# Packing every sign convolution two output channels to a weight, with the precision check moved out of the main path

## The chip, the core and the metric

The program runs on one core of a Trainium2 chip. The metric is the device time of the whole launch in microseconds; the kernel before takes 1131.07 us (median of three runs, 1129.95 to 1135.38). The engines that matter are TensorE (matmuls, and the weight loads that go with them), ScalarE (activations; ACT in the profile), VectorE (DVE), GpSimd (POOL) and the DMA queues. They run side by side and wait for one another through semaphores.

## What is computed

Four layers are applied to x of shape (16, 256, 28, 28): 16 images, 256 channels, 784 pixels. Cut to what matters here:

```python
# layer 0: 3x3 convolution of signs by signs, batch norm, residual
y = conv3x3(sign(x), sign(w0)) * mean(|w0|)
x = batchnorm(y) + x
# layer 1: 3x3 and 1x1 convolutions with real weights, gates, PReLU (not touched by the change)
# layer 2: two more sign-by-sign convolutions
o = sign(batchnorm(x));  o = prelu(conv3x3(o, sf1 * sign(w1)), a1)
o = sign(batchnorm(o));  o = prelu(conv3x3(o, sf2 * sign(w2)), a2)
x = prelu(batchnorm(o) + x, a3)              # prelu(v, a) = v if v >= 0 else a * v
# layer 3: single-head attention over the 784 pixels, softmax, projection, residual
x = x + Wp @ softmax(q^T k / 8) v
```

Batch norm takes mean and variance over all images, so a layer must be finished for every image before the next can start. In a sign-by-sign convolution each output is a whole number of magnitude at most 2304 (256 channels by 9 taps).

## The kernel before

The 256 input channels are two blocks of 128 (k), the 256 outputs two blocks of 128 (mo), and a 3x3 convolution is nine shifted matmuls per block. An image is worked in two halves of 392 pixels; `j` counts the 32 half images. The nine taps by two blocks make six chunks `n` of three taps.

Five of the six chunks are *packed*: the weight `4095 * sign(w of channel o+128) + sign(w of channel o)` gives two output channels in one matmul, `4095 b + a`. To take it apart, ScalarE computes `r = ps/4095` plus a large constant, so that the addition rounds to the whole number b; VectorE subtracts the constant; and two more matmuls, by matrices -4095 I and I, add `-4095 b` to the packed sum (which leaves a) and put b in the second bank. The sixth chunk is *plain*, so that the packed sum cannot grow beyond what fp32 holds exactly: three matmuls for each of the two output blocks.

```python
    def sign_layer(pads, w, temp, sign, post, steps, moments, first=None, together=1):
        def packed(*js):
            for j in js:
                pss[j] = conv_ps()                        # two PSUM banks, three such pairs in all
            for n in range(5):
                for j in js:
                    for t in range(3):
                        product(j, 0, w[0][:, n, t, :], n, t, n + t == 0, n + t == 6)
            for j in js:
                r, bs[j] = temp("t1"), temp("uv", FR)
                A.activation(r, pss[j][:, 0, :HN], AF.Identity, bias=rounding, scale=1.0 / PACK)
                V.tensor_scalar(bs[j], r, -ROUND, None, ALU.add)
        def plain(j):
            for mo in range(2):
                for t in range(3):
                    product(j, mo, w[1][:, t, mo * P:(mo + 1) * P], 5, t, ...)
            for mo in range(2):
                T.matmul(pss[j][:, mo, :HN], lhsT=unpack[mo], rhs=bs[j], ...)
        ...
            for j in range(2 * B + 1):                    # cut: the order of the engines' work
                packed(j)
                if j > 0:
                    plain(j - 1); post(j - 1, pss[j - 1])
                sign_image(j // 2 + 1)                    # every second j: signs of the next image
                if j == 2 * B - 2: moments.gather()
                if late: late()
                late = steps.pop(0)() if j >= 2 and steps else None   # weights of the next layers
```

After that `post` takes what it needs from PSUM. In layer 0 it is two `bn_stats` and an int16 copy; in layer 2 the PReLU as `y + (1 - a) * relu(-y)` and the statistics:

```python
            def post0(j, ps):                             # layer 0
                for mo in range(2):
                    V.bn_stats(mom.part(j, mo), ps[:, mo, :HN])
                A.copy(ns[b][:, :, h * HN:(h + 1) * HN], ps[:, :, :HN])
                def post(j, ps):                          # layer 2, both convolutions
                    A.activation(r[:, mo], ps[:, mo, :HN], AF.Relu, scale=-1.0)
                    for mo in range(2):
                        V.scalar_tensor_tensor(p, r[:, mo], beta[:, mo:mo + 1], ps[:, mo, :HN], ALU.mult, ALU.add)
                        V.bn_stats(mom.part(j, mo), p)
```

Beside layer 0 run the `steps`: six that prepare layer 1's weights (`w1_step`: ten VectorE and four ScalarE operations), six sums of |w0|, one for the 1x1 weights, one for constants, and five of the six chunks of the next sign layer's weights. Matmuls on zeros (`keep_busy`) fill the gaps between layers.

The attention begins with layer 2's last norm, residual and PReLU for each image (`finish_a`, `_b`, `_c`). From image 2 on the residual is added by a DMA that accumulates into SBUF. The finished image is also stored to DRAM (`xd`), for a second version of the attention that runs in a branch if the exponentials overflowed:

```python
    def finish_a(b, ...):   # ACT: norm; b < 2: DVE adds x2; b >= 2: DMA with accum adds x2d
    def finish_b(b, ...):   # ACT: rl = relu(-x)
    def finish_c(b, ...):   # DVE: x = rl * (1 - a3) + x;  SP: dma xd[b] <- x
        for b in range(B - 1):                            # cut
            scores(b, 1)
            if b == 0: finish_b(1); finish_c(1)
            sum_up(b, 1); scores(b, 2); scores(b, 3); sum_up(b, 2, 3)
            queries_keys(b + 1, ...); keys_to(...); queries(...)
            if b == 0: finish_a(2)
            project_v(b + 1); turn_v(b + 1)
            scores(b, 4); scores(b, 5); sum_up(b, 5)
            finish_b(b + 2); finish_c(b + 2); finish_a(b + 3)
            for c in range(4): values(b, c)
            ...
```

Of the kernel before, what the change touches and what calls it, by code (L numbers as in the profile page):

```python
# [35 lines left out]
P = 128  # L37
# [12 lines left out]

ROUND = 1.5 * 2**23
# [12 lines left out]

@with_exitstack
def conv_seq_kernel(ctx: ExitStack, tc: tile.TileContext, d: dict, out: bass.AP):
# [28 lines left out]
    CHUNKS = [(k, g) for g in range(3) for k in range(2)]  # L95

    unpack = [wpool.tile([P, P], FR, name=f"unpack{i}") for i in range(2)]
    rounding = const.tile([P, 1], F32, name="rounding")
# [22 lines left out]
    class Moments:  # L121


        def __init__(self, name, early, late, early_count):
            self.parts = const.tile([P, 2, early, 6], F32, tag="parts", name=name + "_parts")
            self.fin = const.tile([P, 2, 3 + 6 * late], F32, name=name + "_fin")
            self.mv = const.tile([P, 2, 2], F32, name=name + "_mv")
            self.early, self.count = early, float(early_count)
# [4 lines left out]
        def gather(self):  # L133

            nc.gpsimd.memset(self.fin[:, :, 0:1], self.count)
            for k in range(2):
                V.bn_aggr(self.fin[:, k, 1:3], self.parts[:, k].rearrange("p c s -> p (c s)"))
            V.tensor_scalar(self.fin[:, :, 2:3], self.fin[:, :, 2:3], self.count, None, ALU.mult)

# [32 lines left out]
    def packed_weights(pool, **kw):  # L172
        return pool.tile([P, 5, 3, P], FR, name="wpk", **kw)

    def plain_weights(pool, **kw):
        return pool.tile([P, 3, 256], FR, name="wpl", **kw)
# [14 lines left out]
    def sign_weights(pool, dst, src, total, acc, stage=("st", 2), tmp=None, ab_tag="rn", sg=("sg", 1)):  # L191
# [9 lines left out]
        def sign(k, g):  # L201
            st = sts[k, g]
            n = CHUNKS.index((k, g))
            if n == 5:
                A.activation(dst[1], st, AF.Sign, saturate=False)
                return lambda: None
# [3 lines left out]
                dst[0][:, n], t[:, :, P:], PACK, t[:, :, 0:P], ALU.mult, ALU.add  # L210
# [33 lines left out]
    def sign_layer(pads, w, temp, sign, post, steps, moments, first=None, together=1):  # L244
# [4 lines left out]
        bs = [None] * 2 * B  # L249

        def product(j, mo, lhsT, n, t, start, stop, again=False):
            k, g = CHUNKS[n]
            r, c = divmod(3 * g + t, 3)
            r += HR * (j % 2)
            T.matmul(  # L255
                pss[j][:, mo, :HN].rearrange("p (a b) -> p a b", b=S), lhsT=lhsT,
                rhs=pads[:, j // 2 % 2, k, r:r + HR, c:c + S], start=start, stop=stop, skip_group_check=again,
            )

        def packed(*js):  # L260
            for j in js:
                pss[j] = conv_ps()
            for n in range(5):
                for j in js:
                    for t in range(3):
                        product(j, 0, w[0][:, n, t, :], n, t, n + t == 0, n + t == 6)
            for j in js:
                r, bs[j] = temp("t1"), temp("uv", FR)
                A.activation(r, pss[j][:, 0, :HN], AF.Identity, bias=rounding, scale=1.0 / PACK)  # L269
                V.tensor_scalar(bs[j], r, -ROUND, None, ALU.add)  # L270

        def plain(j):
            for mo in range(2):
                for t in range(3):
                    product(j, mo, w[1][:, t, mo * P:(mo + 1) * P], 5, t, mo == 1 and t == 0, False, mo == 0)
            for mo in range(2):
                T.matmul(  # L277
                    pss[j][:, mo, :HN], lhsT=unpack[mo], rhs=bs[j], start=False, stop=True, skip_group_check=(mo == 0)
                )
# [7 lines left out]
        with tc.manual_schedule(engines={ET.PE, ET.Activation, ET.DVE, ET.SP}):  # L287
            for j in range(2 * B + 1):
                if j == 0:
                    sign_image(0)  # L290
                    if first:
                        first()
                if j == 0:
                    packed(*range(together))
                elif together <= j < 2 * B:
                    packed(j)
                if j > 0:
                    plain(j - 1)
                    post(j - 1, pss[j - 1])
                if j == 0:  # L300
                    sign_image(1)
                elif j % 2 == 0 and j // 2 + 1 < B:
                    sign_image(j // 2 + 1)
# [4 lines left out]
                late = steps.pop(0)() if j >= 2 and steps else None  # L308
        assert not steps and not late
# [18 lines left out]
    w0 = [packed_weights(wpool, tag="wa"), None]  # L328
# [13 lines left out]
    with tc.tile_pool(name="ps_conv", bufs=3, space=PSUM) as psc, \  # L342
# [13 lines left out]
        with tc.tile_pool(name="ph1", bufs=1) as ph:  # L356

            fpads = float_pads(ph, "vs")
            w0[1] = plain_weights(ph, tag="z2", bufs=1)
# [18 lines left out]
            def temp(tag, dt=F32):  # L378
                return ph.tile([P, HN], dt, tag=tag, name=tag, bufs=2)
# [15 lines left out]
            eye = ph.tile([P, P], F32, tag="rn", name="eye", bufs=4)  # L395
            make_identity(nc, eye)
            for u, f in zip(unpack, (-PACK, 1.0)):
                V.tensor_scalar(u, eye, f, None, ALU.mult)
            nc.gpsimd.memset(rounding, ROUND)
# [58 lines left out]
            def constants():  # L458
                v = const.tile([P, 4, 2], F32, name="v_bn")
# [26 lines left out]
            w2a = [packed_weights(wpool, tag="wa2"), None]  # L486
            signs2, sums2 = sign_weights(xpool, w2a, d["w2a"], sf1, pss, ("x2", 3), tmp=ph)

            steps = load_ahead(steps + both(signs2, sums2)[:5], 2)
# [5 lines left out]
            def post0(j, ps):  # L495
# [3 lines left out]
                for mo in range(2):  # L499
                    V.bn_stats(mom.part(j, mo), ps[:, mo, :HN])  # L500
                A.copy(ns[b][:, :, h * HN:(h + 1) * HN], ps[:, :, :HN])  # L501
# [355 lines left out]
            with tc.manual_schedule(engines={ET.PE, ET.DVE, ET.Activation}):  # L857
                sc0, bi0 = norm("l0", mom, pv("g0"), pv("b0"), sf0, first)
                zb1 = tt(vtile("zb1"), bi0, pv("a_move"), ALU.add)
# [91 lines left out]
        with tc.tile_pool(name="ph2", bufs=1) as ph:  # L951
            w2b = [packed_weights(ph, tag="wb"), plain_weights(ph, tag="wbl")]
            w2a[1] = plain_weights(ph, tag="wal")
            fpads = float_pads(ph, "fpads")

            def temp(tag, dt=F32):
                return ph.tile([P, HN], dt, tag=tag, name=tag, bufs=2)

            rest = [x[5] for x in sign_weights(ph, w2a, d["w2a"], sf1, pss, ("r", 2), ab_tag="ab")]
            rest[0].load()  # L960
# [26 lines left out]
            r1, r2 = combine("r1", pv("a1"), -1.0, 1.0), combine("r2", pv("a2"), -1.0, 1.0)  # L987

            def post2(order, beta, mom):

                def post(j, ps):
                    i, h = divmod(j, 2)
                    r = ph.tile([P, 2, HN], F32, tag="r", name="r", bufs=2)
                    for mo in (slice(0, 1), slice(1, 2)) if j == 2 * B - 1 else (slice(0, 2),):
                        A.activation(r[:, mo], ps[:, mo, :HN], AF.Relu, scale=-1.0)  # L995
                    for mo in range(2):
                        p = pt[order[i]][:, mo, h * HN:(h + 1) * HN]
                        V.scalar_tensor_tensor(p, r[:, mo], beta[:, mo:mo + 1], ps[:, mo, :HN], ALU.mult, ALU.add)  # L998
                        V.bn_stats(mom.part(j, mo), p)
                return post  # L1000

            steps = both(*sign_weights(xpool, w2b, d["w2b"], sf2, pss, ("x2", 3), tmp=ph, ab_tag="ab"))
# [560 lines left out]
```

## Time and profile before

| stretch of the span, us | what runs | PE busy | DVE busy | ACT busy | granted clock |
|---|---|---|---|---|---|
| 10.70 to 153.50 | layer 0, sign convolution | 142.64 | 81.33 | 78.70 | 1.00 |
| 161.40 to 497.00 | layer 1 | 335.60 | 303.61 | 237.51 | 1.00 |
| 538.00 to 676.00 | layer 2, first sign convolution | 137.97 | 87.52 | 74.73 | 1.00 |
| 688.00 to 827.00 | layer 2, second sign convolution | 139.00 | 82.49 | 73.99 | 1.00 |
| 842.00 to 877.00 | attention, its start | 25.38 | 11.79 | 17.41 | 0.76 |
| 877.00 to 1100.00 | attention, images 2 to 14 | 223.00 | 161.59 | 168.30 | 1.00 |

The profiled execution has a span of 1132.2 us. Each row gives the length of time that each engine was executing something within that stretch; an engine whose busy time equals the stretch never paused. The granted clock is the share of full speed at which TensorE was allowed to run.

### The profile page before, as it was taken

To read this page: it belongs to the slowest core of one execution; us is meant where nothing else is said; L and a number is where in the kernel's file an instruction comes from. 1 tells how busy PE (TensorE), PEld (TensorE's weight loads), DVE (VectorE), ACT (ScalarE), POOL (GpSimd) and SP (SyncE) were. 2 spreads that over 40 slices of the span, in tenths; PEclk is the share of its full clock that TensorE was granted. 3 is DMA by queue.
4 is the path that set the end of the run, shared out by engine and by line. 5 is a ranking of instruction groups with operands and counts; after the bars stand their busy time and mean duration, and the time that the engine had idled before them with its cause. 6 is when DMAs were issued, how large, how long until landed. Compare 5 with 4: busy or idle time off the path is not lost.

```text
span 1132.2 us, 16021 instructions
## 1 busy us (share of the span) xinstructions
PE 1097.7 (97%) x6139; PEld 917.0 (81%) x6139; DVE 807.4 (71%) x1460; ACT 712.5 (63%) x1065; POOL 139.0 (12%) x140
## 2 busy tenths in 40 slices
PE   6999999999999999998999999999986999999996
PEld 6999989999999999994999998999942444444442
DVE  4766369899999999967576565565663677777865
ACT  5555445777777777766465544555554777877762
POOL 2000000000000000001000000000002444344331
PEclk9999999999999999998999999999997999999998
DMA  8554331222321222012560000000004356446522
GB/s 319 203 180 160 129 118 55 72 86 75 126 86 71 100 100 71 29 58 116 196 271 1 1 1 1 1 1 1 1 29 103 90 150 167 128 133 171 147 83 116
DMA packets 26662, 111.64 MB, mean 99 GB/s; under 512 B 3458, under 2 KB 7236, under 8 KB 26580
## 3 DMA queue, kind: packets, MB, share of 16 engines
q1 hardware_dynamic: 20948, 80.01, 19.2%
q0 software_dynamic: 5632, 30.54, 10.0%
q8 instruction: 50, 0.82, 0.3%
q14 instruction: 32, 0.26, 0.1%
HBM read 65.59 MB, written 44.96 MB: 98 GB/s over the span
## 4 chain that ended last, share of the span: by engine, by line
PE 92%; DVE 3%; ACT 2%; issue 1%; DMA 1%; POOL 0%; SPq 0%; ACTq 0%; POOLq 0%; DVEq 0%
PE cv L255 33%; PE cv L599 25%; PE sc L1180 7%; PE av L1201 7%; PE cv L705 4%; PE mi L1157 4%; PE cv L277 3%; PE unused L354 2%; PE sm L1243 2%; PE mi L1259 2%; PE sm L1201 1%; PE sumabs L222 1%; DMA p<-x2d 1%; PE hid L527 1%; PE gate L676 1%
## 5 line engine op out<-in xcount | busy, mean ns | idle before, releaser
L599 PE MATMUL cv<-vs,w 128*128 128x392 f32 x1536 | 301.3, 354 | 0.0
L255 PE MATMUL cv<-fpads,wpk 128*128 128x392 f32 x1440 | 292.0, 355 | 8.5 <-DVE wpk L209 8.3
L599 PEld LDWEIGHTS cv<-vs,w 128*128 128x128 f32 x1536 | 287.1, 190 | 1.6 <-issue 0.3
L255 PEld LDWEIGHTS cv<-fpads,wpk 128*128 128x128 f32 x1440 | 270.6, 191 | 11.0 <-POOL worst L1044 7.8
L998 DVE SCALAR_TENSOR_TENSOR p<-r,r,cv 128x392 f32<-128x392 f32 x128 | 78.5, 613 | 78.5 <-ACT r L995 78.5
L255 PE MATMUL cv<-fpads,wpl 128*128 128x392 f32 x576 | 124.9, 353 | 0.2 <-ACT t L269 0.2
L255 PEld LDWEIGHTS cv<-fpads,wpl 128*128 128x128 f32 x576 | 108.7, 190 | 1.1 <-ACT t L269 0.5
L269 ACT ACTIVATE t<-cv,rounding 128x392 f32<-128x392 f32 x96 | 56.1, 585 | 80.1 <-PE cv L255 77.9
L1184 ACT ACTIVATE es<-sc 128x784 f32<-128x784 f32 x112 | 87.3, 822 | 23.9 <-PE sc L1180 23.0
L1180 PE MATMUL sc<-q,keyswa 64*128 64x392 f32 x448 | 91.6, 521 | 3.0 <-issue 2.4
L995 ACT ACTIVATE r<-cv 128x784 f32<-128x784 f32 (+1 forms) x66 | 52.9, 805 | 56.6 <-PE cv L277 55.2
L1201 PE MATMUL av<-es,v 128*64 128x392 f32 x448 | 81.6, 503 | 5.7 <-ACT es L1184 5.7
L270 DVE TENSOR_SCALAR uv<-t 128x392 fp32r<-128x392 f32 x96 | 35.0, 365 | 71.5 <-ACT t L269 71.4
L1180 PEld LDWEIGHTS sc<-q,keyswa 64*128 64x128 f32 x448 | 39.5, 189 | 47.2 <-issue 27.8
L1201 PEld LDWEIGHTS av<-es,v 128*64 128x64 f32 x448 | 29.4, 137 | 53.4 <-issue 46.8
L1194 POOL TENSOR_TENSOR sum<-sum,es 128x784 f32<-128x784 f32 x32 | 68.0, 2126 | 3.4 <-ACT es L1184 1.0
L104 DVE TENSOR_TENSOR vs<-pad 128x840 fp32r<-128x840 bf16 (+1 forms) x66 | 64.4, 999 | 0.1
L501 ACT CAST n<-cv 128x784 int16<-128x784 f32 x32 | 26.0, 812 | 54.3 <-DVE l_parts L500 18.9
L1168 DVE COPY keyswa<-mi 64x392 f32<-64x392 f32 x31 | 16.3, 564 | 56.0 <-ACT q L1164 56.0
L745 POOL DMA_DIRECT2D x2d<-x x16 | 8.5, 532 | 356.9 <-DVE x L739 294.1
L1157 PE MATMUL mi<-p,wqk 128*128 128x392 f32 x124 | 47.4, 525 | 3.5 <-DVE p L1147 3.5
L705 PE MATMUL cv<-z,fw 128*128 128x392 f32 x256 | 49.2, 343 | 0.8 <-ACT z L697 0.7
(271 smaller groups left out, 1654.4 us busy)
## 6 DMA issues: line engine op xcount, KB each, us to landing
xs<-in_x_dram SPq DMA_DIRECT2D x30, 784.0 KB, 4.3
x2d<-x POOLq DMA_DIRECT2D x16, 784.0 KB, 3.6
xd<-p SPq DMA_DIRECT2D x16, 784.0 KB, 3.3
out_dram<-p SPq DMA_DIRECT2D x15, 784.0 KB, 6.4
p<-x2d POOLq DMA_DIRECT2D x14, 784.0 KB, 8.3
p<-x2d SPq DMA_DIRECT2D x13, 784.0 KB, 7.7
n0d<-n POOLq DMA_DIRECT2D x16, 392.0 KB, 2.7
n<-n0d SPq DMA_DIRECT2D x16, 392.0 KB, 2.9
```

Of the source, the lines that this page charges most:

```text
L104: V.tensor_tensor(o, a, b, op)
L255: T.matmul(pss[j][:, mo, :HN].rearrange("p (a b) -> p a b", b=S), lhsT=lhsT, rhs=pads[:, j // 2 % 2, k, r:r + HR, c:c + S], start=start, s ...
L269: A.activation(r, pss[j][:, 0, :HN], AF.Identity, bias=rounding, scale=1.0 / PACK)
L599: T.matmul(ps.rearrange("p (a b) -> p a b", b=S), lhsT=w[:, k, c, u, mo * P:(mo + 1) * P], rhs=vs[:, b % 2, u, k, :, c:c + S], start=(n == 0),
L705: T.matmul(ps[:, h, :HN], lhsT=w[:, k, mo * P:(mo + 1) * P], rhs=z2[b][:, k, h * HN:(h + 1) * HN], start=(k + i == 0), stop=(k + i == 2),)
L995: A.activation(r[:, mo], ps[:, mo, :HN], AF.Relu, scale=-1.0)
L998: V.scalar_tensor_tensor(p, r[:, mo], beta[:, mo:mo + 1], ps[:, mo, :HN], ALU.mult, ALU.add)
L1157: T.matmul(ps[:, h, :HN], lhsT=wqk[:, k, :], rhs=x[b][:, k, h * HN:(h + 1) * HN], start=(k == 0), stop=(k == 1))
L1180: T.matmul(ps[:, h, :HN], lhsT=chunk[rows], rhs=qs[b][rows], start=True, stop=True)
L1184: A.activation(e, ps[:, :, :HN], AF.Exp, scale=0.125)
L1194: (V if late else nc.gpsimd).tensor_tensor(sums[b, late], sums[b, late], e, ALU.add)
L1201: T.matmul(ps[64 * h:64 * h + 64, :HN], lhsT=w, rhs=e[:, h, :], start=start, stop=stop)
```

## The change

All six chunks become packed; the plain products and the two unpacking matmuls go. ScalarE now rounds and then subtracts the constant (two activations), and VectorE computes `a = ps - 4095 b` into SBUF beside b. `post` works from SBUF. The packed sum can now, for extreme data, exceed what comes apart exactly; the kernel therefore gathers sums of squares of a (layer 0: from the statistics, on GpSimd; layer 2: a ScalarE `Square` with accumulation per half image), and at the end, together with the overflow test of the attention, decides whether a whole careful version of the network (`careful=True`: two groups of three chunks, and the shifted attention) must run in a branch. With the given inputs that branch is not taken.

PReLU becomes `max(a * y, y)`, one VectorE operation, without the relu on ScalarE (it needs slopes of at most 1, which the test includes). The store of `xd` goes out of the main path. In the attention's start, the norm of image 2 and its accumulating DMA are issued earlier, the residual add and PReLU of image 1 are earlier in VectorE's order, and eight idle matmuls are put in.

```diff
+def conv_seq_kernel(tc, d, out):
+    again = forward(tc, d, out, False)
+    with tc.If(again > 0):
+        forward(tc, d, out, True)
...
-        return pool.tile([P, 5, 3, P], FR, name="wpk", **kw)
+        return pool.tile([P, 6, 3, P], FR, name="wpk", **kw)
...
+        groups = 2 if careful else 1
+        size = 6 // groups
+        def products(*js):
+            for j in js:
+                pss[j] = conv_ps()
+            for n, (k, g) in enumerate(CHUNKS):
+                for j in js:
+                    for t in range(3):
+                        T.matmul(pss[j][:, n // size, :HN]..., lhsT=w[:, n, t, :], rhs=pads[...], ...)
+        def apart(j):
+            for g in range(groups):
+                t, ab, ps = temp("t1"), temp(), pss[j][:, g, :HN]
+                A.activation(t, ps, AF.Identity, bias=rounding, scale=1.0 / PACK)
+                A.activation(ab[:, 1], t, AF.Identity, bias=unrounding)
+                V.scalar_tensor_tensor(ab[:, 0], ab[:, 1], -PACK, ps, ALU.mult, ALU.add)
...
+            sign_image(0)
+            for j in range(2 * B):
+                products(j)
+                if j % 2 == 0 and j // 2 + 1 < B:
+                    sign_image(j // 2 + 1)
+                if j > 0:
+                    post(j - 1, abs_[j - 1])
+                if j == 2 * B - 2: moments.gather()
+                if late: late()
+                late = steps.pop(0)() if j >= 2 and steps else None
+                apart(j)
+            post(2 * B - 1, abs_[2 * B - 1])
...
-                    V.bn_stats(mom.part(j, mo), ps[:, mo, :HN])
-                A.copy(ns[b][:, :, h * HN:(h + 1) * HN], ps[:, :, :HN])
+                    V.bn_stats(mom.part(j, mo), ab[:, mo])
+                A.copy(ns[b][:, :, h * HN:(h + 1) * HN], ab)
...
-                        A.activation(r[:, mo], ps[:, mo, :HN], AF.Relu, scale=-1.0)
-                        V.scalar_tensor_tensor(p, r[:, mo], beta[:, mo:mo + 1], ps[:, mo, :HN], ALU.mult, ALU.add)
+                            V.scalar_tensor_tensor(p, y, alpha[:, mo:mo + 1], y, ALU.mult, ALU.max)
                         V.bn_stats(mom.part(j, mo), p)
+                    if not careful:
+                        A.activation(temp("t2"), ab[:, 0], AF.Square, scale=SAFE**-0.5, accum_out=doubt[:, j:j + 1])
...
-    A.activation(rls[k][:, n], x[b][:, k, n], AF.Relu, scale=-1.0)
-    V.scalar_tensor_tensor(v, rls[k][:, n], na3[:, k:k + 1], v, ALU.mult, ALU.add)
-    nc.sync.dma_start(out=xd[b], in_=x[b])
+            V.scalar_tensor_tensor(v, v, alpha[:, k:k + 1], v, ALU.mult, ALU.max)
...                                                       # attention, order at its start
+        keep_busy(8)
         ...
-            if b == 0: finish_b(1); finish_c(1)
+            if b == 0: finish_a(2)                        # finish_b(1) now stands before the loop
```

All six chunks of the second sign layer's weights are now prepared beside layer 0; before, the sixth was loaded and prepared at the start of layer 2.

## The prediction

> **What bounds the kernel now.** I read the page's first part and its chain, then the busy times cut by stage, then the groups of the sign layers by shape, then the timelines of each engine inside one stage. The page says that TensorE is busy all but 3% of the span and makes up nearly all of the chain:
>
> ```profile
> PE 1097.7 (97%) x6139; PEld 917.0 (81%) x6139; DVE 807.4 (71%) x1460; ACT 712.5 (63%) x1065; POOL 139.0 (12%) x140
> PE 92%; DVE 3%; ACT 2%; issue 1%; DMA 1%; POOL 0%; SPq 0%; ACTq 0%; POOLq 0%; DVEq 0%
> ```
>
> The busy times by stage (columns: PE, weight loads, DVE, ACT, POOL, clock, DMA share, GB/s) show where there is room beside TensorE. Rows: layer 0, layer 1, the two sign convolutions of layer 2, the attention's start, the attention's steady part.
>
> ```profile
> 10.70:153.50 142.80, 142.64 (x768) 141.61 (x769) 81.33 (x207) 78.70 (x129) 8.15 (x15) 1.00 0.52 188
> 161.40:497.00 335.60, 335.60 (x1836) 334.19 (x1836) 303.61 (x569) 237.51 (x332) 7.95 (x17) 1.00 0.22 78
> 538.00:676.00 138.00, 137.97 (x738) 135.66 (x738) 87.52 (x172) 74.73 (x97) 0.00 (x0) 1.00 0.25 96
> 688.00:827.00 139.00, 139.00 (x737) 137.81 (x738) 82.49 (x157) 73.99 (x96) 0.00 (x0) 1.00 0.00 1
> 842.00:877.00 35.00, 25.38 (x142) 10.73 (x142) 11.79 (x11) 17.41 (x25) 8.31 (x6) 0.76 0.32 80
> 877.00:1100.00 223.00, 223.00 (x1474) 103.84 (x1476) 161.59 (x161) 168.30 (x281) 96.35 (x54) 1.00 0.49 136
> ```
>
> In the three sign stages DVE and ACT are busy 53 to 63% of the time, and weight loads follow each other without a gap. So time falls with the number of matmuls until another engine takes over. In layer 1 and the steady attention nothing on TensorE changes. The pitch comes from the timeline of TensorE in the last sign convolution, one half image:
>
> ```profile
> 729.90 3.00 PE L255 MATMUL cv<-fpads,wpk 128*128 128x392 f32 x15
> 732.74 1.29 PE L255 MATMUL cv<-fpads,wpl 128*128 128x392 f32 x6
> 733.87 0.52 PE L277 MATMUL cv<-uv,unpack 128*128 128x392 f32 x2
> 734.22 2.99 PE L255 MATMUL cv<-fpads,wpk 128*128 128x392 f32 x15
> ```
>
> From 729.90 to 734.22 are 4.32 us for 23 matmuls: 0.188 each (the 355 ns of the group is a modelled, pipelined end). The groups give the other engines' prices:
>
> ```profile
> L269 ACT ACTIVATE t<-cv,rounding 128x392 f32<-128x392 f32 x96 | 56.1, 585 | 80.1 <-PE cv L255 77.9
> L998 DVE SCALAR_TENSOR_TENSOR p<-r,r,cv 128x392 f32<-128x392 f32 x128 | 78.5, 613 | 78.5 <-ACT r L995 78.5
> L999 DVE BATCH_NORM_STATS2 l2c_parts<-p 128x6 f32<-128x392 f32 x58 | 33.0, 569 | 2.0
> L968 ACT ACTIVATE fpads<-p,l2b_c,l2b_r 128x784 fp32r<-128x784 f32 x30 | 29.6, 1037 | 0.0
> ```
>
> **What the Trainium skill says.** "TensorE: Matmul & The Clock Gate", section "Back-to-back issue gap", has the spacing in a real stream set by weight load and matmul together; here the loads last 190 ns and the pitch is 188, so it agrees in kind. "ScalarE: Activation LUTs", section "What ACT_TABLE_LOAD costs", gives 186 ns + 0.833 ns per element, 93 ns more for each per-partition operand, and 93 ns of overlap back to back. For 392 elements with a bias that is 606; the trace has 585 from PSUM. The new subtraction reads SBUF; a plain 392-element activation from SBUF takes 531 here, so I estimate 531 + 93 = 624, some 0.6 us after overlap. "TensorE: Matmul & The Clock Gate", section "HAM oscillation", says that TensorE's idle gaps lower its clock; the clock of 0.76 in the attention's start agrees.
>
> **The change, part by part.** *Matmuls:* 15 + 6 + 2 = 23 become 18 a half image, 18 x 0.188 = 3.39 us instead of 4.33. Over 3 x 32 half images this is 96 x 0.94 = 90 us, if TensorE remains the bound.
>
> *Load of the others in layer 2, per half image.* ACT: rounding 0.6, subtraction 0.6, half of an image's signs (1.97 for the pair back to back) 0.98, square 0.45 + 0.19 for its accumulator: 2.85. DVE: 0.6 for a, two pairs of PReLU and statistics at 1.14 a pair in the timeline: 2.9. Both stay under 3.39. There is also a chain across them. In an even half image ACT does signs 1.97, square 0.65, rounding and subtraction 1.2; in the odd one it waits for DVE's a (0.7), then 0.65 and 1.2. Together 6.5 us a pair with semaphores, against 6.8 on TensorE. So TensorE is still the bound, barely. *Second convolution:* TensorE works from 687.92 to 826.84, 138.9 us; after, 32 x 3.39 = 108.5: 30.4 gained. *First convolution:* 537.44 to 681.13, 143.7, which includes six half images that took 4.95 because DVE also prepares weights. After: 108.5 + 6 x 0.36 for the sums by TensorE + some 1 us. In those six DVE needs 2.9 + 1.6 = 4.5 against 3.75, falls behind by 4.5 us in all, and the three pairs of PSUM banks hide all but about 1. 111.7: 32.0 gained.
>
> *Tails of layer 2:* after the last matmul there are now rounding, subtraction, a, then the last PReLUs and statistics behind the aggregation. I count 5.2 us to the last statistic where the timeline has 4.0: 1.2 lost in each convolution.
>
> *Layer 0:* 10.69 to 154.72, 144.0 us. TensorE after: 108.5 + 12 x 0.36 = 112.8. But the six `w1_step`s come every second half image. DVE then has, per pair, 3.2 for the step, 1.0 for a sum, four statistics 2.0, two a 1.2: about 7.5; ACT has signs 1.5, two int16 copies 1.5, four weight copies 1.2, unpacking 2.4, waits 0.8: about 7.5. TensorE has 7.15. With their mutual waits I take 7.6: 6 x 0.45 = 3 us. The constants, some thirty small DVE operations, cost 2 more. 118: 26 gained, less 1.6 because the last statistics come 1.9 us later, partly under idle matmuls: 24.5.
>
> *Attention.* In steady state nothing: TensorE is full, and the relu that leaves ACT and the stores that leave the queue were beside it. The start is another matter:
>
> ```profile
> 853.20 4.29 PE L1157 MATMUL mi<-p,wqk 128*128 128x392 f32 x6 [1.60 <-DVE p L1147]
> 868.61 1.60 ACT L1142 ACTIVATE rl<-p 128x784 f32<-128x784 f32 x2 [5.43 <-DMA p<-x2d]
> 872.83 1.57 PE L1201 MATMUL av<-es,v 128*64 128x392 f32 x4 [5.74 <-ACT es L1184]
> ```
>
> ACT's queue stands behind image 2's accumulating DMA, issued only at 861.68, and the exponentials behind it hold up TensorE. After the change that DMA is issued about 12 us earlier and only DVE waits for it. From the value projection of image 1 (857.42) to that of image 2 (880.63) are 23.2 us, against 16.4 in steady state: 6.8 gained. Image 1's PReLU (two operations of 2.27 us on DVE while POOL adds, 1.11 alone) moves ahead of the wait: some 4.5. Together 11, the higher clock included.
>
> *Small things:* the checks' few GpSimd operations and one reduction lie beside other work; a branch not taken existed before. Zero.
>
> Sum: 24.5 + (32.0 - 1.2) + (30.4 - 1.2) + 11 = 95.5. From 1131.1 this leaves 1035.6; I add 3.5 for small waits that such counts leave out: 1039.
>
> **Rivals.** *A: ACT and DVE become the bound.* The chain of 6.5 us against 6.8 leaves 4%. If the subtraction or the square costs 0.2 more, the pair takes 7.0 to 7.2: 16 x 0.3 = 5 us in each of two or three stages, 1045 to 1055. For it: the first convolution was already DVE-bound in six half images. Against: overlap of back-to-back activations, which the timeline shows (0.47 between starts of a 0.57 activation). *B: layer 0 is held by its side work throughout*, at 4.0 per half image: about 128, 10 us more, 1049. For it: ACT's and DVE's sums are within 5% of TensorE's there. Against: only 12 of 32 half images carry the heavy steps. *C: the attention gains nothing at its start*, because image 1's PReLU still collides with POOL: 1050. *D: it also profits from a clock that stays up*, 4 us more: 1035.
>
> **Range and chances.** A, B and C each cost about 10; two of them together give 1060. All gains and D give 1030. For a time within 2% of the old one, nearly 75 of the 90 us would have to vanish, which only an engine 20% above TensorE could do. So 1024 to 1062; faster 0.97, same 0.02, slower 0.01.
>
> **What would show it.** TensorE's starts of half images 3.4 us apart in the second convolution of layer 2, weight loads still without gaps: right. A pitch of 3.6 or more, with TensorE waiting for PSUM (released by the DVE operation that makes a): A. Layer 0's pairs at 7.6 for the first twelve half images and 6.8 at the end: right; above 8 throughout: B. No wait for the DMA in the attention's start and a clock near 1: right. The prediction as a whole would be wrong if the new activations took much over 0.6 us, or if the second program's presence slowed the first.

## The result and the profile after

The changed kernel takes 1044.1 us (median of four runs, 1042.43 to 1045.54) where the kernel before takes 1130.86 (four runs, 1129.95 to 1135.38): a ratio of 0.9225, with a 95% interval of 0.9197 to 0.9253. The prediction was 1039 with a range of 1024 to 1062. The profiled executions have spans of 1132.2 and 1042.2 us, so they differ by 90.0, where the medians differ by 86.8; the stages below are read from these two. The profiled execution of the kernel before took 1134.12 us, 3.3 above its median (mean granted clock 0.986; executions of 1130.06 and 1130.53 us had 0.991), so that some 3 of the 90.0 us belong to that execution and not to the change; in which stage, the traces don't show.

The page of the changed kernel, its busy times and its chain by engine:

```profile
PE 1007.5 (97%) x5667; PEld 827.9 (79%) x5667; DVE 826.0 (79%) x1460; ACT 729.8 (70%) x1189; POOL 139.4 (13%) x147
...
PE 82%; DVE 9%; ACT 6%; issue 1%; DMA 1%; SPq 0%; POOL 0%; ACTq 0%; POOLq 0%; DVEq 0%
```

472 matmuls are gone (5667 against 6139: 480 fewer in the convolutions, eight idle ones more) and TensorE is still busy 97%. But its share of the chain fell from 92% to 82%, and VectorE and ScalarE together hold 15% instead of 5%: somewhere TensorE no longer sets the time alone. The busy times by stage say where. Columns: length, PE, weight loads, DVE, ACT, POOL, granted clock, DMA share, GB/s. Rows: layer 0, layer 1, the two sign convolutions of layer 2, the attention's start, its steady part.

```profile
10.30:131.80 121.50, 117.50 (x618) 113.06 (x619) 90.95 (x212) 99.58 (x161) 9.49 (x19) 1.00 0.66 226
139.80:476.00 336.20, 336.17 (x1840) 335.05 (x1841) 304.71 (x570) 237.89 (x334) 7.20 (x15) 1.00 0.23 78
515.00:632.80 117.80, 114.37 (x604) 112.37 (x602) 96.38 (x176) 85.80 (x160) 1.01 (x2) 0.99 0.30 116
640.80:750.00 109.20, 109.20 (x576) 108.46 (x576) 87.89 (x154) 82.80 (x155) 0.00 (x0) 1.00 0.00 1
765.00:789.00 24.00, 23.39 (x161) 10.59 (x163) 11.50 (x13) 17.52 (x25) 11.08 (x7) 1.00 0.39 68
789.00:1009.00 220.00, 220.00 (x1468) 102.54 (x1470) 162.41 (x161) 147.21 (x253) 92.60 (x53) 1.00 0.36 89
```

In the second convolution of layer 2 TensorE is busy 109.20 of 109.20. In layer 0 and in the first convolution it pauses 4.0 and 3.4 us. The attention's start now has a clock of 1.00 where it had 0.76.

The timeline of TensorE cut where one stage's first matmul starts gives the ledger (a gap is the time from one layer's last sign matmul, where the idle matmuls begin, to the next layer's first product):

| stretch | before | after | change | predicted |
|---|---|---|---|---|
| layer 0, sign convolution | 144.03 | 121.54 | -22.5 | -26.0 |
| gap to layer 1 | 6.45 | 8.03 | +1.6 | +1.6 |
| layer 1 and its end | 376.27 | 375.28 | -1.0 | 0 |
| layer 2, first sign convolution | 143.69 | 117.65 | -26.0 | -32.0 |
| gap | 6.79 | 8.00 | +1.2 | +1.2 |
| layer 2, second sign convolution | 138.92 | 109.29 | -29.6 | -30.4 |
| gap to the first query product | 9.94 | 10.10 | +0.2 | +1.2 |
| attention, first query product to value projection of image 2 | 43.85 | 28.76 | -15.1 | -11 |
| steady attention | 212.62 | 212.55 | -0.1 | 0 |
| the rest, to the end of the span | 38.95 | 40.74 | +1.8 | 0 |

With 0.4 us less ahead of layer 0 the changes add up to 90.0. The groups by shape give the prices of the new operations (mean ns of one behind the comma, then the idle time before them and who ended it):

```profile
L285 PE MATMUL cv<-fpads,wpk 128*128 128x392 f32 x1728 | 336.6, 356 | 9.2 <-POOL l_fin L152 7.3 <-ACT fpads L982 1.3 <-DVE wpk L232 0.5
L1016 DVE SCALAR_TENSOR_TENSOR p<-ab,vec 128x392 f32<-128x392 f32 x128 | 79.1, 618 | 2.2
L295 ACT ACTIVATE ab<-t,unrounding 128x392 f32<-128x392 f32 x96 | 59.8, 623 | 3.2
L294 ACT ACTIVATE t<-cv,rounding 128x392 f32<-128x392 f32 x96 | 55.4, 577 | 27.1 <-PE cv L285 25.6 <-issue 1.2
L296 DVE SCALAR_TENSOR_TENSOR ab<-ab,cv 128x392 f32<-128x392 f32 x96 | 53.9, 561 | 65.8 <-ACT ab L295 65.4
L1019 ACT ACTIVATE t<-ab 128x392 f32<-128x392 f32 x64 | 33.5, 523 | 26.6 <-DVE ab L296 26.6
```

The new subtraction takes 623 ns; the forecast had 624. The PReLU as a maximum costs VectorE 618 where the old one cost 613, so it saves VectorE nothing; what it saves is the relu on ScalarE and the wait for it. VectorE's `a` (L296) waits 65.4 us in all for ScalarE's subtraction: the two engines work in series.

**What holds the first convolution.** The timeline of all engines in the changed kernel, of which VectorE's and ScalarE's lines from one packing of weights (`wpk`) to the next are kept, with one TensorE wait. Columns: start, length, engine, line, operation; in brackets the idle time before it and who ended it.

```profile
539.26 0.54 DVE L232 SCALAR_TENSOR_TENSOR wpk<-sg 128x384 fp32r<-128x384 bf16 x1
...
539.83 0.84 ACT L231 ACTIVATE sg<-st 128x768 bf16<-128x768 f32 x1 [2.23 <-DVE wpk L232]
540.58 0.57 ACT L294 ACTIVATE t<-cv,rounding 128x392 f32<-128x392 f32 x1
...
540.95 0.58 PE L245 MATMUL sumabs<-ones,ab 128*128 128x1 f32 x4 [0.72 <-DVE ab L239]
541.18 0.62 ACT L295 ACTIVATE ab<-t,unrounding 128x392 f32<-128x392 f32 x1
...
541.84 0.56 DVE L296 SCALAR_TENSOR_TENSOR ab<-ab,cv 128x392 f32<-128x392 f32 x1 [1.03 <-ACT ab L295]
542.43 0.63 DVE L1016 SCALAR_TENSOR_TENSOR p<-ab,vec 128x392 f32<-128x392 f32 x1
...
544.23 0.57 DVE L1017 BATCH_NORM_STATS2 l2b_parts<-p 128x6 f32<-128x392 f32 x1
544.71 0.54 DVE L232 SCALAR_TENSOR_TENSOR wpk<-sg 128x384 fp32r<-128x384 bf16 x1
```

Followed by its releasers this is a ring. The tile of weight signs `sg` has one buffer, so ScalarE may sign the next weights only after VectorE has packed the last ones (2.23 us of waiting); rounding and subtraction stand behind it in ScalarE's order; `a` waits for them (1.03); PReLU and statistics follow, and then the next packing. From 539.26 to 544.71 are 5.45 us for a half image, in which VectorE and ScalarE are busy 4.32 us each (ScalarE 2.57 in the next, which has no image to sign). TensorE needs 3.75, so VectorE would fall behind in any case, but by 0.57 us a half image and not by 1.7.

TensorE first lives on its PSUM banks and then waits at the column sums, 0.72, 1.36 and 1.36 us. After the third wait its 18 products take 5.10 us where they took 3.66 before:

```profile
551.87 0.58 PE L245 MATMUL sumabs<-ones,ab 128*128 128x1 f32 x4 [1.36 <-DVE ab L239]
552.30 5.10 PE L285 MATMUL cv<-fpads,wpk 128*128 128x392 f32 x18
```

The granted clock is 0.50 from 553.3 to 555.3. It costs little here, as the ring turns no faster (the next column sum starts 5.47 us after this one), but it is one reason that the pauses, 3.4 us, are less than the time lost.

### The profile page after: what moved, and what is told of

Same layout as the page of the kernel before. It is cut to its first block, busy times and chain, and to the rows that moved or that the text cites. A ratio compares the mean times of both kernels' runs of the same rounds, so it can differ in the third digit from the quotient of the medians.

```text
span 1042.2 us, 15026 instructions
## 1 busy us (share of the span) xinstructions
PE 1007.5 (97%) x5667; PEld 827.9 (79%) x5667; DVE 826.0 (79%) x1460; ACT 729.8 (70%) x1189; POOL 139.4 (13%) x147
## 4 chain that ended last, share of the span: by engine, by line
PE 82%; DVE 9%; ACT 6%; issue 1%; DMA 1%; SPq 0%; POOL 0%; ACTq 0%; POOLq 0%; DVEq 0%
PE cv L614 27%; PE cv L285 23%; PE sc L1218 8%; PE av L1239 8%; PE cv L720 4%; PE mi L1195 4%; PE sm L1281 2%; PE mi L1297 2%; DVE ab L296 1%; ACT ab L295 1%; DVE p L1016 1%; PE unused L371 1%; ACT t L294 1%; PE sm L1239 1%; DVE l_parts L515 1%
## 5 line engine op out<-in xcount | busy, mean ns | idle before, releaser
L285 PE MATMUL cv<-fpads,wpk 128*128 128x392 f32 x1728 | 336.6, 356 | 9.2 <-POOL l_fin L152 7.3
L285 PEld LDWEIGHTS cv<-fpads,wpk 128*128 128x128 f32 x1728 | 327.5, 192 | 12.1 <-POOL l_fin L152 7.3
L296 DVE SCALAR_TENSOR_TENSOR ab<-ab,cv 128x392 f32<-128x392 f32 x96 | 53.9, 561 | 65.8 <-ACT ab L295 65.4
L1016 DVE SCALAR_TENSOR_TENSOR p<-ab,vec 128x392 f32<-128x392 f32 x128 | 79.1, 618 | 2.2
L295 ACT ACTIVATE ab<-t,unrounding 128x392 f32<-128x392 f32 x96 | 59.8, 623 | 3.2
L1019 ACT ACTIVATE t<-ab 128x392 f32<-128x392 f32 x64 | 33.5, 523 | 26.6 <-DVE ab L296 26.6
L737 ACT ACTIVATE u<-cv,c_bn,s_bn 128x784 f32<-128x784 f32 x30 | 30.1, 1005 | 24.4 <-PE cv L720 24.4
L720 PEld LDWEIGHTS cv<-z,fw 128*128 128x128 f32 x256 | 45.8, 188 | 1.5 <-ACT z L712 1.3
L1195 PE MATMUL mi<-p,wqk 128*128 128x392 f32 x124 | 45.3, 506 | 0.3 <-PE unused L371 0.2
```

The source lines that it names most:

```text
L285: T.matmul(pss[j][:, n // size, :HN].rearrange("p (a b) -> p a b", b=S), lhsT=w[:, n, t, :], rhs=pads[:, j // 2 % 2, k, r:r + HR, c:c + S] ...
L295: A.activation(ab[:, 1], t, AF.Identity, bias=unrounding)
L720: T.matmul(ps[:, h, :HN], lhsT=w[:, k, mo * P:(mo + 1) * P], rhs=z2[b][:, k, h * HN:(h + 1) * HN], start=(k + i == 0), stop=(k + i == 2),)
L1016: V.scalar_tensor_tensor(p, y, alpha[:, mo:mo + 1], y, ALU.mult, ALU.max)
L1195: T.matmul(ps[:, h, :HN], lhsT=wqk[:, k, :], rhs=x[b][:, k, h * HN:(h + 1) * HN], start=(k == 0), stop=(k == 1))
```

## The experiments

**The theories.** Theory 1: the six microseconds missing in the first convolution, and those missing in layer 0, are orders and buffers: the ring over `sg`, TensorE standing in order at the column sums of |w| (`sumabs`), and the three-product weight step beside layer 0. Its rival: VectorE and ScalarE have too much work there, or ScalarE's chain is the bound generally. For the attention's start, theory 1 is the order of the DMA and of image 1's PReLU; its rival is TensorE's clock or the idle matmuls. For the end, a jump over the second program, against slower last work.

### A second buffer for the weight signs

```diff
-  steps = both(*sign_weights(..., ab_tag="sums"))                  # weights prepared beside layer 2's first convolution
+  steps = both(*sign_weights(..., ab_tag="sums", sg=("sg", 2)))
```

> The changed kernel with one thing different: the tile of weight signs beside the first sign convolution of layer 2 has two buffers instead of one. In the changed kernel six half images there take 5.46 us each. Theory 1 (a loop through the single sign tile: ScalarE's weight signs wait for VectorE's packing, then rounding and subtraction follow, then VectorE's a): the six half images fall to 4.5 us, VectorE's own sum, and the convolution from 117.7 us to about 113. Theory 2 (what holds TensorE is VectorE's work with its latencies, whichever buffer is free): 117.7 stays. Total 1039 or 1044.

Measured: 1041.27 us (1037.23 to 1042.23), ratio to before 0.9195 (0.916 to 0.9229). The first convolution, from its first product to the idle matmuls behind it, takes 113.18 instead of 117.65:

```profile
515.87 4.33 PE L285 MATMUL cv<-fpads,wpk 128*128 128x392 f32 x21
629.05 6.65 PE L371 MATMUL unused<-idle 128*128 128x512 bf16 x30
```

The ring is real, and worth 4.5 us: the column sums now stand 4.34 us apart, which is VectorE's own work. The whole fell by 2.8 only, as the profiled execution is 1.4 us longer outside this stage; a difference of this size is read from the stage, not from the medians.

### The column sums one half image later

```diff
-  return lambda: total_up(k, g, ab)                # matmuls with the column sums, next half image
+  return lambda: lambda: total_up(k, g, ab)        # one half image later
...
-  if late: late()
-  late = steps.pop(0)() if j >= 2 and steps else None
+  if later: later()
+  later = late() if late else None
+  late = steps.pop(0)() if j >= 2 and steps else None
```

> The changed kernel with the column sums of the weights' magnitudes (two small matmuls each) issued one half image later in TensorE's order, in layer 0 and in layer 2. Theory 1 (TensorE, in order, stands at such a sum for VectorE's reduction and so can never run more than one half image ahead, the three pairs of PSUM banks notwithstanding): the waits for the reduction (7.2 us) go; the first convolution of layer 2 falls by 4 to 5 us and layer 0 by 3 to 4, total about 1036. Theory 2 (the banks themselves are what TensorE waits for; the sums only show it): the waits move to the products and both stages stay within 1 us, total 1044.

Measured: 1042.83 us, ratio 0.9218 (0.9191 to 0.9245). Layer 0 falls to 119.76 (-1.8), the first convolution to 116.1 (-1.5): less than theory 1 expected. The waits of TensorE from layer 0 to the end of the first convolution, first in the changed kernel and then here (columns: who waited for whom, us in total, times, longest):

```profile
PE sumabs L245 <- DVE ab L239: 7.2, 10, 1.4
```

```profile
PE cv L285 <- DVE ab L296: 2.3, 6, 0.6
...
PE cv L285 <- ACT fpads L984: 1.3, 1, 1.3
...
PE sumabs L245 <- DVE ab L239: 0.3, 1, 0.3
```

Of the 7.2 us, 6.9 went, but only 3.3 arrived. In layer 0 TensorE now waits for `a` to free its PSUM banks (2.1 of the 2.3 us). In the first convolution the ring still turns at its own pace, and TensorE meets it at the next image's signs, which stand behind it in ScalarE's order (1.3 us, at 551.45); the 18 products after that wait take 5.49 us, at a clock of 0.62 from 552.4 to 556.9. The largest wait in the list was the place where the ring showed, not its cause.

### Both

Here the tile of weight signs has two buffers beside layer 0 as well.

> Both together, with two sign tiles in layer 0's weights too. Theory 1: the first convolution of layer 2 comes down to TensorE's own 111 to 112 us (as forecast for the changed kernel), layer 0 from 121.5 to 117; total about 1033. Theory 2: no better than the second tile alone, 1039.

Measured: 1035.56 us (1034.69 to 1035.9), ratio 0.915 (0.9123 to 0.9177). Layer 0 takes 118.02, the first convolution 111.9. Its windows here, layer 0 and the two convolutions:

```profile
10.50:128.50 118.00, 115.93 (x619) 113.43 (x620) 90.75 (x212) 98.72 (x161) 9.51 (x19) 1.00 0.67 231
511.80:623.60 111.80, 111.80 (x602) 111.12 (x600) 95.90 (x175) 85.21 (x158) 0.88 (x2) 1.00 0.32 122
632.00:741.00 109.00, 109.00 (x577) 108.17 (x576) 87.99 (x155) 82.59 (x156) 0.00 (x0) 1.00 0.00 1
```

With the same work (VectorE busy 95.90 us, ScalarE 85.21, against 96.38 and 85.80 in the changed kernel) TensorE never pauses in the first convolution. So it was order, not load; the rival falls for this stage. Layer 0 stays 1 us above what theory 1 expected, with 2.1 us of pauses left.

### The weight step of layer 1 split in two

```diff
   # on top of the two edits above: within one w1_step
-  for u, (w, f) in enumerate(...):                 # hi and lo halves: 4 on ScalarE, 4 on VectorE
-      A.activation(hi, w, AF.Copy, scale=f); V.scalar_tensor_tensor(lo, w, f, hi, ...)
+  def halves_of():                                 # the same work, in the next half image
+      for u, (w, f) in enumerate(...): ...
+  return halves_of
```

> The version with two sign tiles and late column sums (1035.6, layer 0 118.0 us), and each of layer 1's six weight steps cut in two: clip and sums in one half image, the copies and remainders in the next. In the changed kernel a pair of half images with such a step takes 7.96 us, by waits between ScalarE and VectorE. Theory 1 (the waits, since each engine's own sum is about 7.4): the pair falls to about 7.4 and layer 0 to 115, total 1032. Theory 2 (VectorE's sum is the bound): layer 0 stays within 1 us of 118.

Measured: 1032.01 us (1031.1 to 1032.98), ratio 0.9111 (0.9086 to 0.9137). Layer 0 takes 114.31, a pair of half images 7.24 to 7.28:

```profile
10.40:124.60 114.20, 114.20 (x618) 113.34 (x618) 90.45 (x212) 97.82 (x161) 9.50 (x19) 1.00 0.69 239
```

TensorE is busy all of it. What was left in layer 0 was the burst of the weight step in every second half image. This version beats both kernels.

### The PReLU as relu and addition again, in layer 2

```diff
+  A.activation(r2, ab, AF.Relu, scale=-1.0)
-  V.scalar_tensor_tensor(p, y, alpha[:, mo:mo + 1], y, ALU.mult, ALU.max)
+  V.scalar_tensor_tensor(p, r2[:, mo], beta[:, mo:mo + 1], y, ALU.mult, ALU.add)
```

> The changed kernel with layer 2's PReLU put back to two operations, y + (1 - a) relu(-y), the relu on ScalarE over both channels at once, 784 elements from SBUF. Theory 1 (ScalarE and the chain between ScalarE and VectorE are within 5% of TensorE's 3.42 us a half image): with 0.75 us more on ScalarE the pair of half images takes about 7.9 us instead of 6.83; each of the two convolutions of layer 2 gains 12 to 17 us, total about 1072. Theory 2 (the maximum brings nothing, ScalarE has room): 1044.

Measured: 1095.97 us, ratio 0.9681 (0.9649 to 0.9712). TensorE's timeline at the end of the second convolution and up to the first query product:

```profile
781.56 3.68 PE L285 MATMUL cv<-fpads,wpk 128*128 128x392 f32 x18 [0.50 <-DVE ab L296]
785.40 3.69 PE L285 MATMUL cv<-fpads,wpk 128*128 128x392 f32 x18 [0.16 <-DVE ab L296]
789.57 3.68 PE L285 MATMUL cv<-fpads,wpk 128*128 128x392 f32 x18 [0.48 <-DVE ab L296]
793.09 9.89 PE L371 MATMUL unused<-idle 128*128 128x512 bf16 x45
810.70 2.95 PE L1198 MATMUL mi<-p,wqk 128*128 128x392 f32 x4 [7.73 <-DVE p L1185]
```

Starts two half images apart (781.56 and 789.57) are 8.0 us apart, where the changed kernel has 6.83, and TensorE waits for `a` to free its banks. This is what the prediction's rival A describes, brought about by a whole relu (0.86 us an operation); the expected 7.9 was right. The convolutions take 136.6 and 123.9, that is 18.9 and 14.6 more. But the whole lost 52, not 28. Most of the rest is at the layers' ends: the gaps grew from 8.0 to 15.6 and from 10.1 to 17.6, with TensorE waiting 9.0 and 7.7 us behind its idle matmuls. When TensorE is not the bound, it ends ahead of the others, and these must work off what stands in the PSUM banks before the norm is known: the last `a` of the first convolution is made 9.0 us after TensorE's last product (662.58), in the changed kernel 2.3 us after it (635.03). So packing with this relu in place of the maximum gains 34 us; the two together 87.

### Layer 2's check left out

This kernel no longer notices sums that did not come apart: it leaves out the `Square` with its accumulator.

```diff
-  A.activation(temp("t2"), ab[:, 0], AF.Square, scale=SAFE**-0.5, accum_out=doubt[:, j:j + 1])
```

> Leaves out layer 2's check of the sums: the ScalarE Square with its accumulator in each half image, so that the kernel no longer notices sums that did not come apart. Theory 1 (TensorE alone sets the second sign convolution of layer 2, at 18 x 0.19 us a half image): that stretch stays at 109.3 us; the first one, whose six weight half images pass through ScalarE, shrinks by at most 3. Theory 2 (ScalarE's chain within 5% of TensorE is what holds the pitch at 3.415 rather than below): the second convolution falls by 2 us or more, the first by 5 or more.

Measured: 1045.74 us, ratio 0.9235 (0.9204 to 0.9267). TensorE's timeline of the second convolution here:

```profile
641.80 109.44 PE L285 MATMUL cv<-fpads,wpk 128*128 128x392 f32 x576 [1.35 <-ACT fpads L982]
751.08 9.89 PE L371 MATMUL unused<-idle 128*128 128x512 bf16 x45
```

109.28 us, against 109.29; the first convolution takes 117.54, against 117.65. ScalarE's chain, estimated within 4% of TensorE, holds nothing there: theory 1. The check costs no time. Nor does a lighter ScalarE shorten the ring, in which the square has no part.

### The attention's start: the DMA late again

```diff
-  if b == 0: finish_a(2)          # after scores(b, 1)
...
+  if b == 0: finish_a(2)          # ahead of project_v(b + 1), as in the kernel before
```

> The changed kernel with the norm of image 2 and its accumulating DMA put back to where the kernel before had them, after image 1's keys. In the changed kernel the attention's start, from the first query product to the value projection of image 2, takes 28.8 us against 43.9 before. Theory 1 (the early DMA removed the wait for it): a wait for the DMA comes back, on VectorE now, and the stretch grows by 5 to 8 us, total about 1050. Theory 2 (the PReLU without ScalarE already took the DMA out of ScalarE's queue; where it is issued matters little): under 1.5 us, total 1044 to 1045.

Measured: 1048.83 us, ratio 0.9267 (0.924 to 0.9295). The start takes 32.06 instead of 28.76: 3.3 more, between the two forecasts. VectorE does wait 4.3 us for the DMA, but TensorE pauses only 1.20 and 1.55 us, both times for a PReLU. Those of image 1 and image 2 on VectorE, then the additions on GpSimd beside them:

```profile
770.37 2.53 DVE L1182 SCALAR_TENSOR_TENSOR p<-p,vec 128x784 f32<-128x784 f32 x1
...
786.16 3.57 DVE L1182 SCALAR_TENSOR_TENSOR p<-p,vec 128x784 f32<-128x784 f32 x2 [4.27 <-DMA p<-x2d]
```

```profile
770.00 2.06 POOL L1230 TENSOR_TENSOR sum<-es 128x784 f32<-128x784 f32 x1 [14.66 <-ACT es L1222]
...
786.48 2.42 POOL L1230 TENSOR_TENSOR sum<-es 128x784 f32<-128x784 f32 x1 [2.56 <-ACT es L1222]
```

In the changed kernel image 1's PReLU takes 1.03 (at 770.60), and GpSimd's first sum starts at 772.92, because the DMA's issue stands ahead of it in GpSimd's order. With the DMA late, GpSimd adds at 770.00, the PReLU lasts 2.53, and it ends at 772.90, 0.84 after GpSimd's end (770.00 + 2.06). Image 2's second PReLU meets the next addition: it lasts 2.62 of the 3.57 us and ends at 789.73, 0.83 after GpSimd's 788.90. At 1.03 us it would have ended in time for TensorE, which was ready for it at 788.24 (an estimate from these lines and TensorE's). So the late DMA costs TensorE its time through the collisions.

### The attention's start: image 1's PReLU late again

```diff
-  finish_b(1, ks=(0,)); finish_b(1, ks=(1,))      # ahead of the loop
...
+  if b == 0: finish_b(1)                          # in the loop, behind scores(0, 1)
```

> One part of the attention's start undone: image 1's residual add and PReLU stand again inside the loop, behind image 0's second scores, in VectorE's order; the early accumulating DMA of image 2 and the rest of the changed kernel stay. Theory 1 (the gain at the start has two parts, and this one ends a collision of VectorE's PReLU with GpSimd's adds): the PReLU of image 1 takes over 2 us an operation again, and the stretch from the first query product to the value projection of image 2, 28.8 us, becomes 33 to 36; the whole about 1049. Theory 2 (with the early DMA the exponentials are there anyway, and the place of the PReLU costs nothing): 28.8 to 30, the whole within 2 us of the changed kernel.

Measured: 1051.12 us (1048.77 to 1051.28), ratio 0.9268 (0.9237 to 0.9299). The start takes 35.95, 7.2 more: theory 1, at its upper end. VectorE and then GpSimd in this kernel:

```profile
772.63 3.38 DVE L1182 SCALAR_TENSOR_TENSOR p<-p,vec 128x784 f32<-128x784 f32 x1
```

```profile
772.99 2.18 POOL L1230 TENSOR_TENSOR sum<-es 128x784 f32<-128x784 f32 x1
```

Again the second PReLU ends 0.84 us after GpSimd's addition: 776.01 against 775.17. The Trainium skill, "SBUF — State Buffer", section "SBUF: two separate sides", says that VectorE and GpSimd share a pair of SBUF ports, that a VectorE operation with two SBUF inputs contends for it with a GpSimd operation that reads SBUF, and that the loser is blocked for the whole instruction. Both runs agree: the operation is not slowed in proportion, it ends 0.83 to 0.84 us after the other, three times. (The VectorE record starts 0.36 us before GpSimd's here and yet loses; spans on GpSimd are rough, so the trace doesn't settle who came first.) Then the clock (windows of this kernel; columns as above):

```profile
760.00:772.00 12.00, 10.47 (x65) 4.46 (x66) 7.23 (x12) 8.19 (x13) 0.00 (x0) 1.00 0.00 0
772.00:776.00 4.00, 0.69 (x2) 0.06 (x1) 3.96 (x2) 1.51 (x3) 3.53 (x3) 0.91 0.50 74
776.00:783.00 7.00, 6.93 (x40) 3.46 (x42) 0.74 (x3) 2.06 (x5) 3.55 (x2) 0.56 0.37 75
783.00:796.00 13.00, 12.68 (x64) 5.34 (x60) 4.77 (x6) 7.92 (x11) 4.31 (x3) 1.00 0.35 62
```

TensorE's wait for the PReLU is 3.4 us, and for the next 7 us its clock is 0.56: six query products take 4.29 us, and the value projection 2.40 instead of 1.53. The waits of 3.9 us in all (0.56 and 3.38 for the two PReLUs) are paid nearly twice: against the changed kernel TensorE pauses 3.9 us more in the start and is busy 3.3 us longer. The waits of 1.20 and 1.55 us in the run before left the clock at 1.00. The Trainium skill, "TensorE: Matmul & The Clock Gate", section "HAM oscillation", puts the limit at idle gaps of some 3.4 us. The gap here fits, but shorter gaps close together lowered the clock too, and the measurements decide: 0.72, 1.36 and 1.36 us in the first convolution of the changed kernel, and 1.87 and 1.60 us in the attention's start of the kernel before, where the clock is 0.50 from 853.2 to 857.4. What in such a series decides is not shown.

### The idle matmuls of the start left out

```diff
-  keep_busy(8)
```

> The changed kernel without the eight idle matmuls at the attention's start. Theory 1 (the gain there is the order of work): the clock stays at 1.00 and the stretch of 28.8 us changes by less than 1 us. Theory 2 (the gain is TensorE's clock, kept up by the idle matmuls): the clock falls below 0.9 in the stretch and it grows by 3 to 6 us.

Measured: 1044.66 us, ratio 0.9223 (0.9197 to 0.9249). The start takes 28.77, the clock stays at 1.00, and a wait of 1.75 us for the keys stands where the eight matmuls were. They bring nothing here.

### No second program

This kernel leaves out the branch and so the careful version of the network; a case that needs it would not be redone.

```diff
-  again = forward(tc, d, out, False)
-  with tc.If(again > 0):
-      forward(tc, d, out, True)
+  forward(tc, d, out, False)
```

> The changed kernel without the branch: the careful version of the network is left out, the test is still computed. From TensorE's last matmul to the end of the span are 6.2 us before and 7.9 after the change. Theory 1 (the 1.8 us are the jump over a program twice as long): the stretch falls to 6 us or less, total 1042. Theory 2 (they are the store of the last output): 7.9 stays.

Measured: 1041.9 us, ratio 0.9197 (0.9165 to 0.9228). The last pieces of the chain, in the changed kernel (span 1042.2) and here (span 1041.1); `count` is the matmul that sums up the flags:

```profile
1034.26 0.20 PE count L1083 x2
1034.46 0.02 issue
1034.49 0.15 DVE flag L1084
```

```profile
1035.86 0.20 PE count L1081 x2
1036.06 0.02 issue
1036.09 0.15 DVE flag L1082
```

From `count` to the end of the span are 7.94 us in the changed kernel and 5.24 here; the kernel before, which jumps over a shorter program, has 6.15. The ends of the spans agree with theory 1: without the jump 2.7 us go, and 1.8 of these are new. This is one trace of each kernel; the medians lie too close to show it by themselves.

## Why the prediction held, and where not

**Pitch and matmul count: right.** 18 matmuls at 0.1897 us give 3.415 a half image; 3.39 was forecast. The second convolution came within 0.8 us, with TensorE never waiting. The load of the others, and the chain "6.5 us a pair with semaphores, against 6.8 on TensorE", held: without the square nothing changed, and with a relu more on ScalarE it tipped over.

**The first convolution: wrong by 6.0 us, the largest error.** The step that failed is "falls behind by 4.5 us in all, and the three pairs of PSUM banks hide all but about 1". It added up VectorE's work (4.5 us a half image; 4.32 measured) as if VectorE could run through. The ring over the single-buffered `sg` takes 5.46, and TensorE, standing in order at the column sums, could use the banks little. With a second buffer and later column sums the stage takes 111.9, where 111.7 was forecast: the sum described a kernel without the ring.

**Layer 0: 3.5 us short.** The term "I take 7.6" for a pair with the weight step measured 7.96 in the five pairs between 28.89 and 68.67: 1.8 us. The half images with sign weights alone take 3.95 to 4.18 where 3.75 was forecast, five between 80.11 and 100.64: 1.8. Both terms mis-sized the mutual waits; the rest of the stage comes out even. Rival B, 4.0 per half image throughout, did not happen: the pitch at the end is 3.41. Splitting the step, on top of the second buffer and the later sums, brought a pair to 7.24 to 7.28 and the stage to 114.31.

**Tails:** 1.6 and 1.2 us as forecast; the third cost 0.2 instead of 1.2.

**The attention's start: 4.1 us better than forecast in these two traces.** Direction and both causes were right, the sizes were not, and they do not add as assumed. "6.8 gained" for the DMA: putting it back late costs 3.3, through the PReLUs that then meet GpSimd. "Some 4.5" for image 1's PReLU ("1.11 alone" is 1.03 in these traces): putting it back late costs 7.2, as a wait long enough to lower the clock is paid a second time in slow matmuls. Together these are 10.5 of the 15.1 us; the relu gone from ScalarE and the interplay of the two moves remain as candidates for the other 4.6. Against the kernel without the idle matmuls (28.77 us for the stretch, the same matmuls otherwise) the 15.1 come apart another way: TensorE pauses 11.9 us before and 2.8 there, and its matmuls take 31.9 us before and 26.0 there, at clocks of 0.81 and 1.00. So 6 of the 15.1 us are the clock. That is rival D; the sum had "the higher clock included" without a term for it. A part of the 4.1 may lie in the 3 us of the one profiled execution.

**Small things:** "A branch not taken existed before. Zero" was wrong: the longer program to be jumped costs the 1.8 us found at the end. The `Square` cost nothing, as said; the checks on GpSimd were not left out by themselves.

**The sum.** Short by 3.5 + 6.0 + 0.8 + 1.8 = 12.1, better by 4.1 + 1.0 (third tail) + 1.0 (layer 1) + 0.4 (start) + 0.1 = 6.6; that is 5.5 net, by which the two traces stay behind the 95.5 of the sum. The medians stay behind it by 8.7, because of the 3.2 us by which the traces overstate the gain. The 3.5 set aside for small waits covered a part, and 5 us remain. 1039 was near also by luck, because errors of opposite sign met.

## What to carry to other kernels

Before you call an engine free, follow one round of the loop through its releasers with every buffer that has a single copy: a ring of waits can take 5.5 us in which no engine has more than 4.5 us of work. If a change takes work from the bounding engine, look first at what was pushed onto the next two: here one relu more on ScalarE cost 52 of the 87 us. Spread steps that come in bursts, and move what an in-order engine waits for, before you look for less work.

## What the runs showed that was not expected

- A VectorE PReLU with two SBUF inputs beside a GpSimd addition ended 0.83 to 0.84 us after that addition, three times in two runs, and so took 2.53, 2.62 and 3.38 us instead of 1.03.
- A TensorE wait of 3.4 us was followed by a granted clock of 0.56 for 7 us; two waits of 1.20 and 1.55 us, 17 us apart, left it at 1.00. But waits of 0.72, 1.36 and 1.36 us, about 5.5 us apart, brought it to 0.50 for at least 2 us.
- A stage whose bound is not TensorE pays again at its end: 7.6 and 7.5 us for the half images still in PSUM.
- Jumping over a second program of the network's whole length cost 2.7 us at the end of the launch, in one trace of each kernel.
